# Layer norm root on ScalarE and centring on TensorE in the first layer of a two-layer kernel

## The chip, the cores and the metric

The kernel runs on one core of a Trainium2 chip. The metric is the device time of one execution in microseconds, the median of three runs. A core has five engines that work side by side, each in its own program order: TensorE (PE in the profile; PEld is its weight load), VectorE (DVE), ScalarE (ACT), GpSimd (POOL) and SyncE (SP), which here only issues DMAs. They wait for each other at semaphores.

## The reference

The input x is 4 x 384 x 64 x 64 in float32. Two layers follow each other. The change is in the first.

```python
# layer 0: x = x + mamba(group_norm(x)); L = 64*64 tokens, C = 384, DI = 768, 16 states
xn = (xs - mu) * rsqrt(var + 1e-5)          # layer norm of the group norm's output, over C
xb, z = split(xn @ in_proj_w.T)             # 768 and 768
xc = silu(causal_conv4(xb) + conv_b)
dt, Bm, Cm = split(xc @ x_proj_w.T)         # 24, 16, 16
dt = softplus(dt @ dt_w.T + dt_b)
h = exp(dt * A) * h + dt * xc * Bm          # scan over L, 768 x 16 states
y = sum(h * Cm) + xc * D
out = (y * silu(z)) @ out_proj_w.T
# layer 1: x = x + outlook_attention(group_norm(x))
```

## The kernel before

The first layer (`mamba_layer`) cuts the 4096 tokens of each of the 4 images into 17 chunks of TM = 241 tokens, 68 in all. A chunk's scan is cut into NU = 12 units; each has 64 of the 768 channels, 16 states each, spread as 2 x 4 rows of 241 over 128 partitions. The program is one loop over the steps s, one unit each, written out by hand; every engine issues in exactly this order (`InOrder`). In step s:

- DVE does the second half of the inputs of unit s+1 (`s_inputs2`, h<-dxr,bp), then the two scans of unit s (`s_scan`, h<-da,h).
- ScalarE does the decays of unit s+1 (`s_decay`, da<-dtr,aneg, four exponentials into each of two PSUM tiles da0 and da1; a tile is free when the scan that reads it is done), with two small copies for the state.
- POOL multiplies unit s-1 with C (`s_outputs`, h<-h,bc), then makes the first half of the inputs of unit s+2 (`s_inputs`, h<-dxr,bc).
- In odd steps TensorE sums the states of units s-3 and s-2 (`s_sum`: y<-xc,ddiag and 16 products y<-h,ssum). The tile h has five buffers: the inputs that are written next, by POOL in the same step and by DVE in the step after, need a buffer that this sum has read.

Between these lies the front work of later chunks and the end work of an earlier one. The tables `plan` and `ends` say at which step r of a chunk, and in which of six slots of the step (EARLY, READY, SCAN, POOL, MID, LATE), each part is issued; r is counted from two chunks ahead, so that parts of several chunks meet in one step, and below "step 5" means s = 5 modulo 12. The front parts of a chunk are: f_load (x to xt); f_mean, f_center, f_square, f_var, f_root, f_pow, f_rs, f_scale (the norms); f_x, f_z (the input projection, ps_in, two blocks of 128 rows at a time); f_conv (four diagonal products per block, ps_cv); f_silu (two ACT_TABLE_LOADs around the silu of xc and zs); f_bc, f_xd (ps_xd, xd); f_dt (three products of 25 rows, ps_dt, each followed by an exponential, dt<-ps_dt); f_plog, f_dtx (the logarithm into PSUM, ps_lg, and dtx on DVE); f_log, f_spread, f_b. The end parts are e_load, e_project (ps_out, three times, copied to xr by ScalarE) and e_store.

All of these products share one PSUM pool, `pmm`, with the tag "mm" and two buffers: a product waits until the tile two before it has been read. The logarithm's tile ps_lg takes a turn in the same pool.

The group norm is folded into the layer norm: per image, `group_norm_coeffs` gives a scale sc and a bias bi for each channel, `x_coeffs` makes from them the matrix avs, the averaging matrix with its rows scaled by sc. f_mean multiplies xt with avs (three products that add up to the mean), f_center takes the mean from sc * xt on DVE, the bias is added within the square and within f_scale. f_root adds 1e-5 on DVE, f_pow raises to the power -0.5 on POOL, f_rs spreads the root over the partitions by a product, f_scale multiplies on DVE. The first chunk's parts run before the loop, the second chunk's are fitted into its first steps by `catch_up`.

Every operation of the first layer is recorded by one helper, so the profile has it at line 45; the groups are told apart by their tiles. The trace has two records for each float32 product.

Of the kernel before, what the change touches and what calls it, by code (L numbers as in the profile page):

```python
# [7 lines left out]
F32 = mybir.dt.float32  # L8
AF = mybir.ActivationFunctionType
# [3 lines left out]
P = 128  # L13
C = 384
# [65 lines left out]
def mamba_layer(ctx, tc, x, w, x1, sc1, bi1, consts, behind):  # L80
# [66 lines left out]
    def x_coeffs(b):  # L147


        st = [xstats[b][:, cb].rearrange("p a s -> p (a s)") for cb in range(NCB)]  # L150
        sc = small.tile([P, 1], F32, tag="sc0", name="sc0")
        bi = small.tile([P, 1], F32, tag="bi0", name="bi0")
        avs = small.tile([P, P], F32, tag="avs", name="avs")
        bc = small.tile([P, 1], F32, tag="bc0", name="bc0")

        def parts():
            yield from group_norm_coeffs(pe, ve, ae, gp, small, pmm, blk12, mhalf, st, sc, bi)
            ae.mul(avs, avg, sc)
            yield False
            pb = pmm.tile([P, 2, TM], F32, tag="mm", name="pb")  # L160
            pe.matmul(pb[:, 0, 0:1], avg, bi, start=True, stop=True)
            yield True
            ve.scalar_tensor_tensor(bc, pb[:, 0, 0:1], -float(NCB), bi, ALU.mult, ALU.add)

        norms.append([parts(), False])
        coeffs[b] = (sc, avs, bc)

    def norm_part(reads):

# [3 lines left out]
            if norms[0][1] is None:  # L173
                norms.pop(0)

    avg = load("avg", [P, P], wf)
    for i in range(NCB * NX):
        x_stat(0, i, x_load(0, i))

# [72 lines left out]
        if c.n < TM:  # L252
            gp.memset(c.xt[:, :, c.n : TM], 0.0)

    def f_mean(c):
        t = c.t
        c.sc, avs, c.bias = coeffs[c.b]
        c.ps = pmm.tile([P, 2, TM], F32, tag="mm", name="ps_ln")
        for cb in range(NCB):
            pe.matmul(c.ps[:, 0, :t], avs, c.xt[:, cb, :t], start=(cb == 0), stop=(cb == NCB - 1))  # L260

    def f_center(c, u=None):

        t = c.t
        c.u = front.tile([P, NCB, TM], F32, tag="u", name="u", bufs=2) if u is None else u
        ve.scalar_tensor_tensor(
            c.u[:, :, :t],
            c.xt[:, :, :t],
            c.sc,
            c.ps[:, 0:1, :t].to_broadcast([P, NCB, t]),  # L270
            ALU.mult,
            ALU.subtract,
        )

    def f_square(c):
        t, u = c.t, c.u
        c.sq = front.tile([P, NCB, TM], F32, tag="sq", name="sq")
        ae.activation(c.sq[:, :, :t], u[:, :, :t], AF.Square, bias=c.bias)

    def f_var(c):  # L280

# [10 lines left out]
    def f_root(c):  # L292
        n = c.spans[0][1]
        c.vs = front.tile([P, 2], F32, tag="vs", name="vs")
        ve.tensor_scalar_add(c.vs[:n, :], c.pv[:n, :, 0], 1e-5)

    def f_pow(c):
        n = c.spans[0][1]
        gp.tensor_tensor(c.vs[:n, :], c.vs[:n, :], mhalf[:n, :], ALU.pow)

    def f_rs(c):
        c.ps = pmm.tile([P, 2, TM], F32, tag="mm", name="ps_rs")
# [8 lines left out]

    def f_scale(c):
        t, u = c.t, c.u
        ve.scalar_tensor_tensor(
            u[:, :, :t],
            u[:, :, :t],
            c.bias,
            c.ps[:, 0:1, :t].to_broadcast([P, NCB, t]),
            ALU.add,
            ALU.mult,  # L320
        )

    def project(c, jj):
        t = c.t
# [146 lines left out]
    def at(f, *args):  # L471
        def part(c):
            f(c, *args)

        part.f = f
        return part

    plan = {
        (-12, SCAN): [f_load],
        (-10, EARLY): [f_mean],  # L480
        (-10, READY): [f_center],
        (-9, POOL): [f_square],
        (-7, EARLY): [f_var],
        (-7, MID): [f_root],
        (-6, SCAN): [f_pow],
        (-5, READY): [f_rs],
        (-5, SCAN): [f_scale],
        (6, MID): [at(f_x, 0)],
        (8, EARLY): [at(f_z, 0)],
        (8, MID): [at(f_x, 1)],  # L490
        (9, POOL): [at(f_z, 1)],
        (9, MID): [at(f_conv, 0)],
        (10, LATE): [at(f_z, 2)],
        (11, LATE): [at(f_x, 2)],
        (12, SCAN): [at(f_conv, 1)],
        (12, LATE): [at(f_conv, 2)],
        (13, POOL): [at(f_silu, "xc", "zs")],
        (14, POOL): [f_bc],
        (15, EARLY): [f_xd],
        (16, READY): [at(f_dt, 0)],  # L500
        (16, SCAN): [at(f_dt, 1)],
        (17, EARLY): [at(f_dt, 2)],
        (17, READY): [at(f_plog, 0)],
        (17, MID): [at(f_dtx, 0)],
        (18, EARLY): [at(f_plog, 1)],
        (18, SCAN): [at(f_dtx, 1), at(f_plog, 2)],
        (19, READY): [at(f_dtx, 2)],
        (19, POOL): [f_log],
        (19, MID): [f_spread],
        (22, SCAN): [f_b],  # L510
    }

    ends = {
        (-9, READY): [lambda c: e_load(c)],
        (4, READY): [lambda c: e_project(c, 0)],
        (6, EARLY): [lambda c: e_project(c, 1)],
        (6, POOL): [lambda c: e_project(c, 2)],
        (15, EARLY): [lambda c: e_store(c)],
    }

    def chunk(k):
        if k not in live:
            c = live[k] = Chunk()
            c.b, c.ci, c.t0, c.n = chunks[k]
            c.t, c.last = TM, live.get(k - 1)
        return live[k]


    def catch_up(s, when):
        for r, w in sorted(plan):  # L530
            n = 6 * r + w
            if 0 <= n < 6 * 20 and ((n - 40) * 23 // 41 if n < 81 else 23 + (n - 81) * 22 // 36) == 6 * s + when:
                for part in plan[r, w]:
                    f = getattr(part, "f", None)
                    if f is f_silu:
                        silu(first, "zs")
                    if f is not f_x:
                        part(second)
# [176 lines left out]
    w_taps(0, 2)  # L715
    f_mean(first)
    w_bias(0, 2)
    f_center(first)
    f_square(first)
    f_var(first)  # L720
    w_bias(2, 3)
# [10 lines left out]
    ve.reduce_sum(cws, cw, AX.X)  # L732
    ve.tensor_mul(cws, cws, bxz[:, :NJ])
    ve.tensor_add(cbias, cbias, cws)
    f_center(second)
    f_x(first, 1)
    f_square(second)
    f_conv(first, 0)
# [4 lines left out]
    f_rs(second)  # L743
    f_scale(second)
    f_conv(first, 1)
    f_mean(third)
    f_center(third, io.tile([P, NCB, XT], F32, tag="xr", name="u"))
    f_conv(first, 2)
    f_silu(first, "xc")
    f_square(third)  # L750
# [480 lines left out]
def layouts(inputs):  # L1231

    import numpy as np

    g = {k: np.asarray(v) for k, v in inputs.items()}
    c = np.ascontiguousarray

    def inner(v):
        v = v.reshape(NJ, P, *v.shape[1:])
        return c(np.swapaxes(v, 0, 1))  # L1240

    a = {}
# [24 lines left out]
    a["ident"] = np.eye(P, dtype=f)  # L1267
    a["avg"] = np.full((P, P), 1.0 / C, f)
# [26 lines left out]
```

## Time and profile before

| | us |
|---|---|
| median of 3 runs | 6304.97 (6302.08 to 6311.46) |
| profiled execution | 6291.97 |
| its span | 6289.9 |
| first scan starts, last scan ends | 111.2, 5031.1 |
| mean clock of TensorE, share of full | 0.936 |

The profiled execution is 13 us shorter than the median. Its span leaves out 2 us at the ends. The busy time of an engine is the union of its records; a busy PE need not be at its peak. In the view of groups a row ends with the idle time of the engine just before these instructions and with what ended it; in the timeline that stands in brackets.

### The profile page before, as it was taken

To read this page: it belongs to the slowest core of one execution; us is meant where nothing else is said; L and a number is where in the kernel's file an instruction comes from. 1 tells how busy PE (TensorE), PEld (TensorE's weight loads), DVE (VectorE), ACT (ScalarE), POOL (GpSimd) and SP (SyncE) were. 2 spreads that over 40 slices of the span, in tenths; PEclk is the share of its full clock that TensorE was granted. 3 is DMA by queue.
4 is the path that set the end of the run, shared out by engine and by line. 5 is a ranking of instruction groups with operands and counts; after the bars stand their busy time and mean duration, and the time that the engine had idled before them with its cause. 6 is when DMAs were issued, how large, how long until landed. Compare 5 with 4: busy or idle time off the path is not lost. (4 is left out here: it accounts for less than half of the span.)

```text
span 6289.9 us, 113342 instructions
## 1 busy us (share of the span) xinstructions
PE 5605.3 (89%) x40488; PEld 3949.3 (63%) x40488; DVE 5373.2 (85%) x4783; ACT 4985.3 (79%) x11842; POOL 5310.6 (84%) x2047
## 2 busy tenths in 40 slices
PE   6888888898888888888888888998888789999999
PEld 5666666666666666666666666666666455555555
DVE  4999999999999999999999999999999945544444
ACT  3888888888888889888888988889988744445453
POOL 3999999999999999999999999999999933333333
PEclk9999999999989899999999999999999799999999
DMA  4555555555555555545555455555555634455444
GB/s 128 133 136 146 147 132 137 129 133 143 147 132 139 138 133 143 139 130 146 135 145 149 127 135 132 134 139 133 130 132 130 176 132 167 162 172 170 170 163 143
DMA packets 639978, 894.21 MB, mean 142 GB/s; under 512 B 130153, under 2 KB 533915, under 8 KB 639284
## 3 DMA queue, kind: packets, MB, share of 16 engines
q1 hardware_dynamic: 639412, 886.96, 51.4%
q8 instruction: 319, 5.23, 0.4%
q14 instruction: 247, 2.02, 0.1%
HBM read 660.89 MB, written 225.70 MB: 141 GB/s over the span
## 5 line engine op out<-in xcount | busy, mean ns | idle before, releaser
L45 DVE TENSOR_TENSOR_SCAN h<-da,h 128x968 f32<-128x968 f32 x1632 | 3449.1, 2154 | 82.6 <-issue 53.7
L45 ACT ACTIVATE da<-dtr,aneg 128x241 f32<-128x241 f32 x6528 | 3036.5, 465 | 294.2 <-DVE h L45 131.5
L45 POOL TENSOR_TENSOR h<-h,bc 128x1928 f32<-128x1928 f32 x816 | 3231.0, 3960 | 12.3 <-DVE h L45 10.1
L45 POOL TENSOR_TENSOR h<-dxr,bc 128x964 f32<-128x964 f32 x816 | 1628.1, 1995 | 104.7 <-PE y L45 88.0
L45 PE MATMUL ps_in<-u,win 128*128 128x241 f32 x4896 | 1078.6, 374 | 85.9 <-DVE dtx L45 78.8
L45 PEld LDWEIGHTS ps_in<-u,win 128*128 128x128 f32 x4896 | 911.0, 190 | 251.4 <-DVE dtx L45 102.9
L45 POOL TENSOR_TENSOR bd<-ain,own 99x1188 f32<-99x1188 f32 x192 | 413.0, 2180 | 744.9 <-DMA ain<-ad 504.9
L45 DVE TENSOR_TENSOR h<-dxr,bp 128x964 f32<-128x964 f32 x816 | 928.1, 1137 | 101.4 <-PE y L45 87.2
L45 PE MATMUL y<-h,ssum 128*32 128x241 f32 x13056 | 906.1, 405 | 23.8 <-POOL h L45 22.6
L45 PEld LDWEIGHTS y<-h,ssum 128*32 128x32 f32 x13056 | 433.0, 119 | 440.9 <-issue 215.4
L45 PE MATMUL ps_cv<-xb,cdiag 128*128 128x241 f32 x3264 | 694.3, 368 | 6.4 <-ACT neg L45 4.3
L45 PEld LDWEIGHTS ps_cv<-xb,cdiag 128*128 128x128 f32 x3264 | 611.0, 189 | 79.9 <-issue 13.5
L45 PE MATMUL ps_xd<-xc,wx 128*56 128x241 f32 x816 | 304.6, 554 | 322.9 <-ACT xc L45 322.9
L45 PE MATMUL psv<-wv,xp 128*128 128x384 f32 x1728 | 589.3, 492 | 0.8 <-ACT vst L45 0.8
L45 ACT ACTIVATE bd<-ain,own 99x324 f32<-99x324 f32 x704 | 334.6, 555 | 293.9 <-PE ps L45 282.5
L45 PE MATMUL ps_out<-zs,wout 128*128 128x241 f32 (+1 forms) x2448 | 536.6, 368 | 0.0
L45 DVE TENSOR_TENSOR fold<-fold,ps 128x192 f32<-128x192 f32 (+1 forms) x768 | 210.9, 303 | 341.1 <-PE ps L45 328.0
L45 PEld LDWEIGHTS ps_out<-zs,wout 128*128 128x128 f32 x2448 | 469.1, 192 | 36.6
L45 PEld LDWEIGHTS psv<-wv,xp 128*128 128x128 f32 x1728 | 320.5, 190 | 224.5 <-issue 7.5
L45 PEld LDWEIGHTS ps_xd<-xc,wx 128*56 128x56 f32 x816 | 153.5, 197 | 462.9 <-ACT xc L45 348.4
L45 PE MATMUL ps_dt<-xd,wdt 25*128 25x241 f32 x816 | 251.5, 434 | 114.4 <-ACT dt L45 80.9
L45 PE MATMUL y<-xc,ddiag 128*128 128x241 f32 x816 | 278.9, 426 | 9.5 <-DVE zs L45 9.5
(108 smaller groups left out, 5342.9 us busy)
## 6 DMA issues: line engine op xcount, KB each, us to landing
dxr<-dxd SPq DMA_DIRECT2D x1632, 120.5 KB
dtr<-dtd SPq DMA_DIRECT2D x1632, 120.5 KB
bc<-bcd SPq DMA_DIRECT2D x544, 120.5 KB
vin<-vd SPq DMA_DIRECT2D x384, 148.5 KB
vd<-vst SPq DMA_DIRECT2D x93, 576.0 KB
dxd<-dtx SPq DMA_DIRECT2D x272, 180.8 KB
dtd<-dt SPq DMA_DIRECT2D x272, 180.8 KB
xs<-in_x SPq DMA_DIRECT2D x96, 256.0 KB
```

Of the source, the lines that this page charges most:

```text
L45: return self.tc.keep_in_program_order(issue(*args, **kwargs))
```

## The change

The mean is no longer taken away on DVE. For each of the three blocks of channels TensorE makes the centred and scaled value whole: the block's own matrix `own` (identity less average, rows scaled by sc) times its part of xt, plus the matrix `others` (minus the average, scaled) times the two other parts. That is nine products in two PSUM tiles (two blocks and one), which ScalarE fetches into u with the bias added. The square and the scaling lose their bias; the scaling is a plain product. The 1e-5 and the root become a logarithm with the bias eps and an exponential with the scale -0.5, both on ScalarE. The order of parts in `plan` and `ends`, and the formula of `catch_up`, are changed as well.

```diff
-            ae.mul(avs, avg, sc)
+            ae.mul(others, navg, sc)
+            ae.mul(own, cavg, sc)
...
-    def f_mean(c):
-        c.sc, avs, c.bias = coeffs[c.b]
-        c.ps = pmm.tile([P, 2, TM], F32, tag="mm", name="ps_ln")
-        for cb in range(NCB):
-            pe.matmul(c.ps[:, 0, :t], avs, c.xt[:, cb, :t], start=(cb == 0), stop=(cb == NCB - 1))
-    def f_center(c, u=None):
-        ve.scalar_tensor_tensor(
-            c.u[:, :, :t],
-            c.xt[:, :, :t],
-            c.sc,
-            c.ps[:, 0:1, :t].to_broadcast([P, NCB, t]),
-            ALU.mult,
-            ALU.subtract,
-        )
+    def f_mean(c, part=None):
+        for n in (0, 1) if part is None else (part,):
+            own, others, c.bias = coeffs[c.b]
+            c.ps = pmm.tile([P, 2, TM], F32, tag="mm", name="ps_ln")
+            for cb in range(2 * n, min(NCB, 2 * n + 2)):
+                for i in range(NCB):
+                    pe.matmul(
+                        c.ps[:, cb % 2, :],
+                        own if i == cb else others,
+                        c.xt[:, i, :TM],
+                        start=(i == 0),
+                        stop=(i == NCB - 1),
+                    )
+            if part is None:
+                f_center(c, n)
+    def f_center(c, n):
+        cbs = slice(2 * n, min(NCB, 2 * n + 2))
+        ae.activation(c.u[:, cbs, :TM], c.ps[:, : 2 - n, :], AF.Identity, bias=c.bias)
     def f_square(c):
-        ae.activation(c.sq[:, :, :t], u[:, :, :t], AF.Square, bias=c.bias)
+        ae.activation(c.sq[:, :, :t], u[:, :, :t], AF.Square)
     def f_root(c):
-        ve.tensor_scalar_add(c.vs[:n, :], c.pv[:n, :, 0], 1e-5)
+        ae.activation(c.vs[:n, :], c.pv[:n, :, 0], AF.Ln, bias=eps[:n])
     def f_pow(c):
-        gp.tensor_tensor(c.vs[:n, :], c.vs[:n, :], mhalf[:n, :], ALU.pow)
+        ae.activation(c.vs[:n, :], c.vs[:n, :], AF.Exp, scale=-0.5)
     def f_scale(c):
-        ve.scalar_tensor_tensor(u, u, c.bias, c.ps ..., ALU.add, ALU.mult)
+        ve.tensor_mul(u[:, :, :t], u[:, :, :t], c.ps[:, 0:1, :t].to_broadcast([P, NCB, t]))
...
     plan = {
-        (-12, SCAN): [f_load],
-        (-10, EARLY): [f_mean],
-        (-10, READY): [f_center],
-        (-9, POOL): [f_square],
+        (-11, READY): [f_load],
+        (-10, EARLY): [at(f_mean, 0)],
+        (-10, READY): [at(f_center, 0), at(f_mean, 1)],
+        (-10, POOL): [at(f_center, 1)],
+        (-8, READY): [f_square],
         (-7, EARLY): [f_var],
-        (-7, MID): [f_root],
-        (-6, SCAN): [f_pow],
+        (-7, READY): [f_root],
+        (-7, SCAN): [f_pow],
...
-        (6, MID): [at(f_x, 0)],
+        (7, MID): [at(f_x, 0)],
...
-        (9, MID): [at(f_conv, 0)],
-        (10, LATE): [at(f_z, 2)],
-        (11, LATE): [at(f_x, 2)],
+        (9, MID): [at(f_z, 2)],
+        (10, LATE): [at(f_conv, 0)],
+        (11, MID): [at(f_x, 2)],
         (12, SCAN): [at(f_conv, 1)],
-        (12, LATE): [at(f_conv, 2)],
-        (13, POOL): [at(f_silu, "xc", "zs")],
-        (14, POOL): [f_bc],
-        (15, EARLY): [f_xd],
+        (12, MID): [at(f_conv, 2)],
+        (14, READY): [at(f_silu, "xc", "zs")],
+        (15, READY): [f_bc],
+        (15, SCAN): [f_xd],
         (16, READY): [at(f_dt, 0)],
         (16, SCAN): [at(f_dt, 1)],
-        (17, EARLY): [at(f_dt, 2)],
+        (16, MID): [at(f_dt, 2)],
         (17, READY): [at(f_plog, 0)],
-        (17, MID): [at(f_dtx, 0)],
-        (18, EARLY): [at(f_plog, 1)],
+        (17, MID): [at(f_dtx, 0), at(f_plog, 1)],
...
-        (19, POOL): [f_log],
         (19, MID): [f_spread],
+        (19, LATE): [f_log],
...
     ends = {
-        (-9, READY): [lambda c: e_load(c)],
-        (4, READY): [lambda c: e_project(c, 0)],
-        (6, EARLY): [lambda c: e_project(c, 1)],
+        (-9, LATE): [lambda c: e_load(c)],
+        (4, EARLY): [lambda c: e_project(c, 0)],
+        (6, READY): [lambda c: e_project(c, 1)],
         (6, POOL): [lambda c: e_project(c, 2)],
-        (15, EARLY): [lambda c: e_store(c)],
+        (14, READY): [lambda c: e_store(c)],
     }
```

More of the change, by code (lines that the diff above doesn't have):

```diff
@@ L152, in x_coeffs @@
         bi = small.tile([P, 1], F32, tag="bi0", name="bi0")
-        avs = small.tile([P, P], F32, tag="avs", name="avs")
+        others = small.tile([P, P], F32, tag="others", name="others", bufs=1)
+        own = small.tile([P, P], F32, tag="own", name="own", bufs=1)
         bc = small.tile([P, 1], F32, tag="bc0", name="bc0")
@@ L157, in parts @@
             yield from group_norm_coeffs(pe, ve, ae, gp, small, pmm, blk12, mhalf, st, sc, bi)
-            ae.mul(avs, avg, sc)
+            ae.mul(others, navg, sc)
+            ae.mul(own, cavg, sc)
             yield False
             pb = pmm.tile([P, 2, TM], F32, tag="mm", name="pb")
-            pe.matmul(pb[:, 0, 0:1], avg, bi, start=True, stop=True)
+            pe.matmul(pb[:, 0, 0:1], navg, bi, start=True, stop=True)
             yield True
-            ve.scalar_tensor_tensor(bc, pb[:, 0, 0:1], -float(NCB), bi, ALU.mult, ALU.add)
+            ve.scalar_tensor_tensor(bc, pb[:, 0, 0:1], float(NCB), bi, ALU.mult, ALU.add)
         norms.append([parts(), False])
-        coeffs[b] = (sc, avs, bc)
+        coeffs[b] = (own, others, bc)
     def norm_part(reads):
@@ L174, in norm_part @@
                 norms.pop(0)
-    avg = load("avg", [P, P], wf)
+    navg = load("navg", [P, P], wf)
+    cavg = load("cavg", [P, P], wf)
     for i in range(NCB * NX):
@@ L253, in f_load @@
             gp.memset(c.xt[:, :, c.n : TM], 0.0)
-    def f_mean(c):
-        t = c.t
-        c.sc, avs, c.bias = coeffs[c.b]
-        c.ps = pmm.tile([P, 2, TM], F32, tag="mm", name="ps_ln")
-        for cb in range(NCB):
-            pe.matmul(c.ps[:, 0, :t], avs, c.xt[:, cb, :t], start=(cb == 0), stop=(cb == NCB - 1))
-    def f_center(c, u=None):
-        t = c.t
-        c.u = front.tile([P, NCB, TM], F32, tag="u", name="u", bufs=2) if u is None else u
-        ve.scalar_tensor_tensor(
-            c.u[:, :, :t],
-            c.xt[:, :, :t],
-            c.sc,
-            c.ps[:, 0:1, :t].to_broadcast([P, NCB, t]),
-            ALU.mult,
-            ALU.subtract,
-        )
+    def f_mean(c, part=None):
[14 more added lines that the diff above has]
+    def f_center(c, n):
+        if n == 0 and c.u is None:
+            c.u = front.tile([P, NCB, TM], F32, tag="u", name="u", bufs=2)
+        cbs = slice(2 * n, min(NCB, 2 * n + 2))
+        ae.activation(c.u[:, cbs, :TM], c.ps[:, : 2 - n, :], AF.Identity, bias=c.bias)
     def f_square(c):
@@ L313, in f_scale @@
         t, u = c.t, c.u
[L314 to L321, printed above, removed]
+        ve.tensor_mul(u[:, :, :t], u[:, :, :t], c.ps[:, 0:1, :t].to_broadcast([P, NCB, t]))
     def project(c, jj):
@@ L524, in chunk @@
             c.b, c.ci, c.t0, c.n = chunks[k]
-            c.t, c.last = TM, live.get(k - 1)
+            c.t, c.last, c.u = TM, live.get(k - 1), None
         return live[k]
@@ L531, in catch_up @@
             n = 6 * r + w
-            if 0 <= n < 6 * 20 and ((n - 40) * 23 // 41 if n < 81 else 23 + (n - 81) * 22 // 36) == 6 * s + when:
+            if 0 <= n < 6 * 20 and ((n - 40) * 22 // 43 if n < 83 else 22 + (n - 83) * 23 // 34) == 6 * s + when:
                 for part in plan[r, w]:
@@ L717, in mamba_layer @@
     w_bias(0, 2)
-    f_center(first)
     f_square(first)
@@ L734, in mamba_layer @@
     ve.tensor_add(cbias, cbias, cws)
-    f_center(second)
     f_x(first, 1)
@@ L745, in mamba_layer @@
     f_conv(first, 1)
+    third.u = io.tile([P, NCB, XT], F32, tag="xr", name="u")
     f_mean(third)
-    f_center(third, io.tile([P, NCB, XT], F32, tag="xr", name="u"))
     f_conv(first, 2)
@@ L1267, in layouts @@
     a["ident"] = np.eye(P, dtype=f)
-    a["avg"] = np.full((P, P), 1.0 / C, f)
+    a["navg"] = np.full((P, P), -1.0 / C, f)
+    a["cavg"] = np.eye(P, dtype=f) - np.full((P, P), 1.0 / C, f)
     a["blk12"] = np.kron(np.eye(P // 4, dtype=f), np.full((4, 4), 1.0 / 12.0, f)).astype(f)
```

## The prediction

> **What bounds the kernel now.** I read the page's busy times first, then the busy time by stretch, then the totals of waits, then one chunk in order of time, last the granted clock in windows of that chunk. The change touches only the first layer: its 816 units, twelve to a chunk, run from about 111 to 5036 us.
>
> Page, busy times, and the steady stretch of the first layer by windows (columns: PE, PEld, DVE, ACT, POOL busy, clock, DMA):
>
> ```profile
> PE 5605.3 (89%) x40488; PEld 3949.3 (63%) x40488; DVE 5373.2 (85%) x4783; ACT 4985.3 (79%) x11842; POOL 5310.6 (84%) x2047
> ```
> ```profile
> 3000.00:4000.00 1000.00, 880.91 (x5816) 654.22 (x5815) 972.52 (x736) 898.50 (x2180) 988.55 (x355) 0.94 0.53 137
> ```
>
> In the stage that changes four engines are at 88 to 99%. POOL looks like the bound, so the square root that leaves it looks like the gain. The totals of waits (us, times, longest) speak against it:
>
> ```profile
> ACT da L45 <- DVE h L45: 131.5, 211, 3.9
> ...
> POOL h L45 <- PE y L45: 88.0, 91, 8.1
> DVE h L45 <- PE y L45: 87.2, 108, 6.3
> ...
> PE ps_in L45 <- DVE dtx L45: 78.8, 66, 5.3
> ```
>
> POOL itself waits for TensorE's sums y, once or more per chunk, and DVE waits for the same sums. A chain through several engines sets the pace. One chunk in order of time shows it:
>
> ```profile
> 3024.97 1.96 ACT L45 ACTIVATE da<-dtr,aneg 128x241 f32<-128x241 f32 x4 [0.65 <-DVE h L45]
> ...
> 3037.06 3.99 PE L45 MATMUL ps_xd<-xc,wx 128*56 128x241 f32 x12 [4.96 <-ACT xc L45]
> ...
> 3041.95 4.24 DVE L45 TENSOR_TENSOR_SCAN h<-da,h 128x968 f32<-128x968 f32 x2 [0.78 <-issue]
> ...
> 3051.81 0.56 ACT L45 ACTIVATE dt<-ps_dt 128x482 f32<-128x482 f32 x1
> ...
> 3052.42 1.08 PE L45 MATMUL ps_dt<-xd,wdt 25*128 25x241 f32 x4 [0.36 <-ACT dt L45]
> ...
> 3054.51 2.98 PE L45 MATMUL y<-h,ssum 128*32 128x241 f32 x32
> ...
> 3057.54 1.16 DVE L45 TENSOR_TENSOR h<-dxr,bp 128x964 f32<-128x964 f32 x1
> ...
> 3064.69 0.65 DVE L45 TENSOR_TENSOR dtx<-ps_lg,xc 128x482 f32<-128x482 f32 x1
> ...
> 3065.40 2.71 PE L45 MATMUL ps_in<-u,win 128*128 128x241 f32 x12 [1.14 <-DVE dtx L45]
> ...
> 3070.77 1.16 DVE L45 TENSOR_TENSOR h<-dxr,bp 128x964 f32<-128x964 f32 x1 [0.43 <-PE y L45]
> ...
> 3070.91 1.98 POOL L45 TENSOR_TENSOR h<-dxr,bc 128x964 f32<-128x964 f32 x1 [0.56 <-PE y L45]
> ...
> 3096.38 1.96 ACT L45 ACTIVATE da<-dtr,aneg 128x241 f32<-128x241 f32 x4 [0.66 <-DVE h L45]
> ```
>
> The loop, with medians over 52 chunks of the same timeline: (a) from the end of a chunk's first scan ScalarE runs without a pause, through the silu and its two table loads, to the second exponential of dt: 27.42 us. (b) TensorE then makes the third dt product and the sum of step 5: 1.86 + 4.07 (means 1.67 + 4.18 = 5.85). (c) DVE, released by that sum, goes from the input of step 6 to the third dtx: 7.81. (d) The third dtx frees the PSUM buffer for f_x(0), which stands ahead of the sum of step 7: 5.43 until DVE's next input. (e) DVE alone to the next chunk's first scan: 25.57. Together 72.2, and the median period is 72.0 us. POOL's own instructions start every 3.90 + 1.95 us back to back, 70.2 per chunk, 70.9 with the power of 0.70: it has 1.1 us of slack, which is its wait for y. DVE's instructions, start to start, make 69.6.
>
> **Off the loop: worth nothing while the loop holds.** POOL loses the power (702 ns, one per chunk); 0.66 us start to start, only more waiting for y. DVE loses the centring (955 ns) and the addition of 1e-5 (130 ns); both stand where it waits later anyway, for decays after the silu (0.78 us above) or for the sum of step 5. The scaling becomes a plain product of 723 elements; the row of 964 (1137 ns) gives 0.85, of 482 (646 ns) 0.97, against 0.94 now: no difference. TensorE makes nine centring products instead of three. Twelve records of ps_in start 2.4 us after each other, so a product costs 0.40, six 2.4; they lie in the 4.96 us in which it waits for the silu, and without that cover they would delay the sum of step 3, which has about 2.5 us to spare. The logarithm and exponential of 121x2 stand on ScalarE behind the end of (a); nearest row 128x3 at 297 ns, about 0.2 start to start, twice 0.4 at most, in front of decays that finish before DVE needs them, and ScalarE waits 1.27 us per chunk for ps_out just behind. Four more scalings of a 128x128 matrix, 0.39 each, are 1.6 us in all.
>
> **Steps moved without a price.** The load of x stands between the same two fetches on SP's queue. The silu and f_xd stay in the same gaps of (a), so their order changes and not its length. The store of dtd goes out behind the eight spreads (4.5 us of SP's time) instead of ahead of them, so the first dtr behind it now waits for its landing; the spreads no longer wait for the logarithm, which gives the time back. Were that not enough, decays would wait for dtr, which they do for 1.8 us in the whole run now. The projections f_z(2) and f_conv(0) change places inside one window of products. e_load is read a chunk later. The third dt product goes ahead of the variance, which matters below.
>
> **On the loop, per chunk.**
> 1. (a) gains the two fetches from PSUM. xb, 482 elements without a bias, takes 0.46 start to next; a bias adds 0.09 (zs 448 ns against xr 355, both 241), so 0.55; the second is like zs, 0.34. The square loses its bias, -0.09. Sum +0.80 (0.6 to 1.0 by the same rows with all or none of the overlap).
> 2. (b): the variance now stands between the second exponential and the sum of step 5, because it takes the PSUM buffer which that exponential frees. It costs 1.43 at full clock, 2.3 to 2.5 in the chunks whose records fall at half clock. The sum takes 2.35 at steps 7 and 9, 4.54 wholly at half clock. The window view, on the clock's own grid, shows why it is slow here:
>
> ```profile
> 3050.06:3053.47 3.41, 3.04 (x21) 2.29 (x19) 3.41 (x3) 3.25 (x9) 3.41 (x2) 1.00 0.89 232
> 3053.47:3056.89 3.42, 3.42 (x27) 1.63 (x30) 3.42 (x4) 3.29 (x8) 3.42 (x2) 0.50 0.84 218
> ```
>
> A window of dt products (25 rows) and variances (one column) is followed by one at half clock, though its records cover 3.04 of 3.41 us. In the new order the last full-array work, ps_out of step 4, starts sooner after the sum of step 3 and ends some 7 us before the sum of step 5; only dt and the variance lie between. That is two windows, so I put the variance at half clock (2.4) and the sum partly so (3.0 to 4.5, mid 3.85): 6.25 against 5.85, +0.40. Bounds: both at half 7.0, +1.2; both at full 3.8, where DVE's own row of work from the scan of step 3 (15.4 us) comes last instead, and (a) and (b) together end 0.3 earlier than now.
> 3. (d): f_x(0) is behind the sum of step 7, so the third dtx is followed by ps_rs and the sum (0.6 + 2.35), and DVE's two scans and scaling (4.15 + 0.87) come last: 5.03 against 5.43, -0.40.
> 4. (c) and (e) stay. From the sum of step 7 to that of step 9 TensorE now has 24 products for 18; 24 at 0.40 and the sum end 22.8 us after the input of step 6, DVE asks at 23.6.
>
> Sum: 0.80 + 0.40 - 0.40 = +0.80 us per chunk, 66 periods: +53. The start adds some 2 (six products at full or half clock 2.4 to 4.8, less the power, the addition and the centring, 1.8; the load of one more matrix). +55 on the profiled execution (span 6289.9, 6291.97 in all) gives 6347; the median of the runs stands 13 above that execution, so 6360.
>
> The Trainium skill, in TensorE: Matmul & The Clock Gate, Part 1, says that the clock halves after an idle window of about 3.4 us and returns after a busy one. Taken as a rule on idle time it would keep the window above at full speed, make the sum of step 5 2.35 us long, and the change would come out at about 44 us faster; the row at 0.50 decides for me.
>
> **Rivals.** First, the clock stays full at step 5, or the variance is done early: DVE's own row comes last, (a) and (b) -0.3, (d) -0.4, so -0.7 x 66 + 2 = -44, 6261. It decides if variance and sum take under about 4.7 us. Against it: all steady sums of step 5 take 3.75 to 4.54. Chance 0.13. Second, POOL is the bound after all: 0.66 x 66 = 44 less with its waits kept, up to 110 less if they go too (72.0 to 70.3). For it: 98.9% busy; against it: it waits in most chunks for a sum that does not wait for POOL. 0.05. Third, the three terms cancel within 0.2% (12.6 us, about what a measurement of this kernel tells from no change): 0.10. Fourth, the cold end: variance and sum all at half clock, or the sum of step 9 late by the 0.8 us that it has: 1.6 x 66 + 2 = +108, 6413; that is part of the forecast's side, in all 0.72. That the change does not do what it says is no rival: in the built order the power is gone from POOL, the nine products stand on TensorE and both fetches on ScalarE.
>
> The range goes from 6275, most of the way to the first rival, to 6410, near the cold end. Faster 0.18, same 0.10, slower 0.72.
>
> **What would show it.** Right: ScalarE's stretch (a) near 28.2; ps_var right behind the second dt exponential and at half clock; the sum of step 5 over 3.5 us; no ps_in waiting for dtx; POOL's and DVE's waits for y larger at step 5 and gone at step 7; a period near 72.8. Wrong: a period under 72 with the clock full at step 5, or POOL back to back at 70.3 without waits, or waits at step 9.

## The result and the profile after

| | before | after |
|---|---|---|
| median of 4 runs, us | 6303.52 (6295.44 to 6311.46) | 6400.2 (6399.19 to 6400.93) |
| profiled execution, its span, us | 6291.97, 6289.9 | 6399.19, 6397.4 |
| mean clock of TensorE | 0.936 | 0.925 |

The ratio is 1.0158, 95% interval 1.0145 to 1.0171: the change makes the kernel 97 us slower by the medians. The spans differ by 107.5 us; that is what the traces have to explain, since the profiled execution of before lies 12 us under its median and that of after does not. The last scan ends 108.2 us later than before and the second layer takes as long as it did, so all of it is in the first layer.

The page of after, busy times, and below it the steady stretch by windows (PE, PEld, DVE, ACT, POOL busy, clock, DMA):

```profile
PE 5759.4 (90%) x41304; PEld 4136.3 (65%) x41304; DVE 5303.0 (83%) x4647; ACT 5074.0 (79%) x12118; POOL 5265.8 (82%) x1979
```
```profile
3000.00:4000.00 1000.00, 894.85 (x5850) 676.95 (x5849) 933.64 (x690) 892.66 (x2175) 954.45 (x332) 0.92 0.51 134
```

POOL and DVE did lose work (45 and 70 us) and the kernel is slower: in the steady stretch they are busy for 954 and 934 of 1000 us where it was 989 and 973. The totals of waits of after say for whom they now wait (us, times, longest):

```profile
POOL h L45 <- PE y L45: 223.7, 78, 9.9
...
DVE h L45 <- PE y L45: 165.9, 79, 7.3
...
ACT xr L45 <- PE ps_out L45: 161.3, 76, 3.8
...
PE ps_var L45 <- ACT dt L45: 76.3, 64, 1.5
PE ps_rs L45 <- DVE dtx L45: 76.2, 63, 6.8
...
PE ps_xd L45 <- ACT u L45: 24.7, 3, 8.2
```

POOL's wait for the sums y went from 88.0 to 223.7 us, DVE's from 87.2 to 165.9. The row of ps_in that waited for dtx (78.8) is gone; ps_rs, which now stands first behind the third dtx, waits instead. The last row, three long waits, belongs to the starts of images. One chunk of after in order of time:

```profile
3020.88 1.96 ACT L45 ACTIVATE da<-dtr,aneg 128x241 f32<-128x241 f32 x4 [0.65 <-DVE h L45]
...
3038.43 4.24 DVE L45 TENSOR_TENSOR_SCAN h<-da,h 128x968 f32<-128x968 f32 x2 [2.22 <-issue]
3040.26 0.45 ACT L45 ACTIVATE u<-ps_ln,bc 128x241 f32<-128x241 f32 x1
...
3048.54 0.56 ACT L45 ACTIVATE dt<-ps_dt 128x482 f32<-128x482 f32 x1
...
3049.16 2.60 PE L45 MATMUL ps_var<-onesc,sq 128*121 128x1 f32 x12 [1.46 <-ACT dt L45]
...
3051.62 1.15 PE L45 MATMUL y<-xc,ddiag 128*128 128x241 f32 x2
...
3052.70 3.02 PE L45 MATMUL y<-h,ssum 128*32 128x241 f32 x32
...
3055.76 1.16 DVE L45 TENSOR_TENSOR h<-dxr,bp 128x964 f32<-128x964 f32 x1 [1.83 <-PE y L45]
3055.89 1.98 POOL L45 TENSOR_TENSOR h<-dxr,bc 128x964 f32<-128x964 f32 x1 [2.98 <-PE y L45]
...
3062.91 0.66 DVE L45 TENSOR_TENSOR dtx<-ps_lg,xc 128x482 f32<-128x482 f32 x1
...
3063.71 0.68 PE L45 MATMUL ps_rs<-ident,vs 121*128 121x121 f32 x4 [1.38 <-DVE dtx L45]
...
3068.42 1.16 DVE L45 TENSOR_TENSOR h<-dxr,bp 128x964 f32<-128x964 f32 x1
```

TensorE has nothing to do for 1.46 us until the second exponential of dt is done (3048.54 + 0.56). From there to DVE's next input (3055.76) the loop is TensorE's: the variance takes 2.60 us and the sum 4.1. In before the variance stood ahead of the third dt product and took 1.43:

```profile
3050.63 1.43 PE L45 MATMUL ps_var<-onesc,sq 128*121 128x1 f32 x12
3052.42 1.08 PE L45 MATMUL ps_dt<-xd,wdt 25*128 25x241 f32 x4 [0.36 <-ACT dt L45]
3053.43 1.16 PE L45 MATMUL y<-xc,ddiag 128*128 128x241 f32 x2
```

The clock in windows over the same place (the last window of 1.00 and the two behind it; clock is the column ahead of the DMA share):

```profile
3044.90:3048.31 3.41, 2.15 (x8) 1.32 (x8) 3.41 (x3) 3.31 (x9) 3.41 (x2) 1.00 0.77 204
3048.31:3051.73 3.42, 2.57 (x13) 2.57 (x13) 3.42 (x3) 3.04 (x8) 3.42 (x2) 0.50 1.06 234
3051.73:3055.14 3.41, 3.41 (x31) 1.57 (x34) 2.20 (x2) 3.25 (x10) 1.18 (x1) 0.50 0.96 221
```

In this chunk the variance and all but the last 0.6 us of the sum run at half clock, and POOL goes from 3.41 us busy in a window to 1.18. In the mean of 52 chunks TensorE spends 8.1 us at half clock between the first dt product and the end of the sum of step 5; before it was 5.4.

The loop of the prediction, medians over the same 52 chunks, means in brackets; (b) is parted into the time to the sum and the sum. Medians of parts need not add up: (b) as a whole is 6.26 (5.85) before and 7.03 (6.87) after.

| us per chunk | before | after |
|---|---|---|
| (a) first scan to second dt exponential | 27.42 (27.51) | 28.27 (28.74) |
| (b) from there to the sum of step 5 | 1.86 (1.67) | 2.51 (2.50) |
| (b) the sum | 4.07 (4.18) | 4.52 (4.36) |
| (c) DVE's input of step 6 to third dtx | 7.81 (7.85) | 7.81 (7.85) |
| (d) third dtx to DVE's next input | 5.43 (5.48) | 4.86 (4.91) |
| (e) to the next chunk's first scan | 25.57 (25.38) | 25.56 (25.35) |
| period | 72.01 (72.11) | 73.20 (73.75) |

Set against each other chunk by chunk from the ends of the first scans, the 108.2 us are: 6.7 until the first scan, 2.4 in the first period, 25.2 in the six periods around the starts of images 2 to 4, 76.0 in the other 60 periods (1.27 each), and -2.1 behind them.

### The profile page after: what moved, and what is told of

It is laid out like the page before. It is cut to its first block, busy times and chain, and to the rows that moved or that the text cites. A ratio compares the mean times of both kernels' runs of the same rounds, so it can differ in the third digit from the quotient of the medians.

```text
span 6397.4 us, 115178 instructions
## 1 busy us (share of the span) xinstructions
PE 5759.4 (90%) x41304; PEld 4136.3 (65%) x41304; DVE 5303.0 (83%) x4647; ACT 5074.0 (79%) x12118; POOL 5265.8 (82%) x1979
## 5 line engine op out<-in xcount | busy, mean ns | idle before, releaser
L45 POOL TENSOR_TENSOR h<-dxr,bc 128x964 f32<-128x964 f32 x816 | 1622.7, 1989 | 294.6 <-PE y L45 223.7
L45 DVE TENSOR_TENSOR h<-dxr,bp 128x964 f32<-128x964 f32 x816 | 931.9, 1142 | 175.7 <-PE y L45 165.9
L45 PE MATMUL ps_in<-u,win 128*128 128x241 f32 x4896 | 1060.0, 372 | 4.6 <-ACT xb L45 3.7
L45 PE MATMUL y<-h,ssum 128*32 128x241 f32 x13056 | 864.4, 410 | 14.6 <-POOL h L45 14.6
L45 PEld LDWEIGHTS y<-h,ssum 128*32 128x32 f32 x13056 | 416.3, 120 | 408.8 <-issue 232.5
L45 PE MATMUL ps_xd<-xc,wx 128*56 128x241 f32 x816 | 265.5, 496 | 228.1 <-ACT xc L45 203.4
L45 PEld LDWEIGHTS ps_xd<-xc,wx 128*56 128x56 f32 x816 | 135.1, 173 | 344.9 <-ACT xc L45 227.7
L45 PE MATMUL ps_dt<-xd,wdt 25*128 25x241 f32 x816 | 236.1, 417 | 39.0 <-ACT xr L45 33.6
```

The lines of the kernel that those rows point to most:

```text
L45: return self.tc.keep_in_program_order(issue(*args, **kwargs))
```

## The experiments

All times are medians in us. Each ratio is against runs of the kernel before that were made beside it, with its 95% interval.

**One part alone: f_x(0) behind the sum of step 7.**

```diff
-        (6, MID): [at(f_x, 0)],
+        (7, MID): [at(f_x, 0)],
```

> The kernel before with one line of the plan changed: f_x(0) behind the sum of step 7 instead of ahead of it. The loop theory: the stretch from the third dtx to DVE's next input falls from 5.43 to 4.9 us, POOL's waits for y at step 7 go, the chunk's period falls from 72.0 to 71.5, 30 to 36 us faster (ratio 0.994 to 0.996). Rival, POOL is the bound and its waits only move: same, within 6 us. Rival, the 24 products between the sums of steps 7 and 9 make the sum of step 9 late: slower, up to 30 us.

Measured 6289.58, ratio 0.9973 (0.9962 to 0.9983): a gain, about half of what was expected. (d) fell to 4.92, as it should; (b) grew from 5.85 to 6.23 by the means. Half-clock time between the first dt product and the end of the sum rose from 5.4 to 6.3 us. The half us that the move saves at step 7 is partly paid back at step 5.

**One part alone: the root on ScalarE, in its old slots.**

```diff
-        ve.tensor_scalar_add(c.vs[:n, :], c.pv[:n, :, 0], 1e-5)
+        ae.activation(c.vs[:n, :], c.pv[:n, :, 0], AF.Ln, bias=eps[:n])
...
-        gp.tensor_tensor(c.vs[:n, :], c.vs[:n, :], mhalf[:n, :], ALU.pow)
+        ae.activation(c.vs[:n, :], c.vs[:n, :], AF.Exp, scale=-0.5)
```

> The kernel before with the root alone changed: logarithm and exponential on ScalarE in the slots of the addition on DVE and of the power on POOL, centring and order as before. The loop theory: off the loop, period 72.0 as before, within 8 us of before; POOL's instructions are 0.66 us less per chunk and its waits for y at step 7 longer by about that. Rival, POOL is the bound: 0.66 x 66 = 44 us faster (ratio 0.993). Rival, ScalarE's busy time is the bound: two instructions of some 0.2 us, 26 us slower.

Measured 6411.47, ratio 1.0172 (1.0152 to 1.0192): a miss, and as slow as the whole change. Its loss is in (c), 7.85 to 9.61 by the means. Three totals of waits of this kernel show how (in before the first is 92.6 us, the second 5.7, and the third is not there):

```profile
ACT xr L45 <- PE ps_out L45: 257.4, 71, 4.6
...
DVE dtx L45 <- ACT ps_lg L45: 129.1, 62, 12.7
...
PE ps_out L45 <- ACT vs L45: 103.4, 64, 2.1
```

The logarithm at step 5, MID, stands on ScalarE behind decays. It is what frees the PSUM buffer of ps_var, and the ps_out of step 6 needs that buffer. So ps_out comes late, ScalarE waits for it with its copy to xr, the logarithms of dt behind that copy come late, and DVE waits for them with dtx. A tiny operation (0.26 us) on a fuller queue became the releaser of a shared buffer.

**The same, in the slots that the change gives it.**

```diff
-        (-7, MID): [f_root],
-        (-6, SCAN): [f_pow],
+        (-7, READY): [f_root],
+        (-7, SCAN): [f_pow],
```

> The kernel before with the root on ScalarE as in before_root, but in the slots of the changed kernel: the logarithm ahead of the first ps_lg, the exponential between the two decays of step 5. In before_root ps_out waited for ScalarE's logarithm, which held the PSUM buffer of the variance; here the buffer is free 2 us sooner. The loop theory: within 10 us of before. Rival, POOL is the bound: 44 us faster. Rival, the root on ScalarE is dear by itself: 100 us slower as before_root.

Measured 6305.13, ratio 1.0003 (0.9993 to 1.0013). POOL loses its power and its wait for y grows by about as much (0.80 to 1.54 us per chunk at step 7, 0.40 to 0.59 at step 5). That POOL bounds the kernel falls with this run, and the root is worth nothing, where its slot is right.

**The change without its centring**: group norm and centring back on DVE as before, with the new order of parts and the root on ScalarE. The lines of the plan, against the kernel after:

```diff
-        (-10, EARLY): [at(f_mean, 0)],
-        (-10, READY): [at(f_center, 0), at(f_mean, 1)],
-        (-10, POOL): [at(f_center, 1)],
+        (-10, EARLY): [f_mean],
+        (-10, READY): [f_center],
```

> The changed kernel with centring and folding of the group norm as before (three products for the mean, DVE centres, bias in square and scaling); the root on ScalarE and the new order stay. The loop theory against the changed kernel (6400): ScalarE's stretch from the first scan to the second dt exponential goes from 28.27 back to 27.4, and the two fetches no longer hold up the start of an image: 0.85 x 66 = 56 us, and 15 to 25 us for three image starts, 6320 to 6335. The variance behind the second dt exponential stays (2.5 us and a sum of 4.4 us at half clock), so it remains 15 to 35 us slower than before. Rival, the new order costs all of it: 6400. Rival, the centring was a gain and the order hid it: above 6400.

Measured 6336.27, ratio 1.0049 (1.0034 to 1.0064). The time is a microsecond above the range that was expected. The centring is 1.1% of the 1.6%. In the loop (a) is back at 27.72 and (b) stays at 2.51 + 4.52. That (a) does not come back to 27.42 is the order of parts: without the fetches ScalarE waits 0.20 us per chunk for scans within (a), in before 0.01. The last scan ends 60.6 us earlier than in after; 31.8 of these are in the 60 steady periods, 19.3 around the image starts, 9.5 at the start. So nearly half of what the centring costs is not in the loop.

**The change with the third dt product behind the variance again.**

```diff
-        (16, MID): [at(f_dt, 2)],
+        (17, EARLY): [at(f_dt, 2)],
```

> The changed kernel with one step moved back: the third dt product stands behind the variance again. The loop theory against the changed kernel (6400): between the second dt exponential and the sum of step 5 stand 1.1 to 2.0 us instead of 2.5; if the clock stays at half, the sum takes 4.1 to 4.5 as now; 0.5 to 1.4 us per chunk, 33 to 90 us faster, 6310 to 6367. Rival, busy time of the engines decides (nothing is removed): 6400. Rival, only the two fetches cost: 6400.

Measured 6358.65, ratio 1.0083 (1.0067 to 1.0099). This one line is worth 0.75%. (b) falls to 1.95 + 4.26 and the period to 72.91 (73.14 by the mean, 73.75 with the whole change). TensorE's rows of one chunk in order of time:

```profile
3023.82 1.08 PE L45 MATMUL ps_dt<-xd,wdt 25*128 25x241 f32 x4 [0.57 <-ACT xr L45]
3024.98 2.60 PE L45 MATMUL ps_var<-onesc,sq 128*121 128x1 f32 x12
3027.52 1.97 PE L45 MATMUL ps_dt<-xd,wdt 25*128 25x241 f32 x4
```

The variance is done in the time in which TensorE stood idle, in this chunk at half clock all the same (2.60; the median over the chunks is 1.84), and what is left behind the second exponential is here a dt product of 1.97 us and the sum. Most of the gain is that time to the sum, 1.95 for 2.50 by the means; the sum itself goes from 4.36 to 4.23.

**The change with its second fetch right behind the first.**

```diff
-        (-10, READY): [at(f_center, 0), at(f_mean, 1)],
-        (-10, POOL): [at(f_center, 1)],
+        (-10, READY): [at(f_center, 0), at(f_mean, 1), at(f_center, 1)],
```

> The changed kernel with the second fetch right behind the first, ahead of the silu, instead of behind the decays of step 2. At the start of an image the group norm's product takes a turn in the two PSUM buffers, so that ps_xd waits for the second fetch: periods of 79.5 and 76.7 us among 73.2, three times each in the run. The loop theory: these fall to some 74, 20 to 30 us in all; ScalarE's stretch keeps its length, so the other periods stay at 73.2; 6370 to 6380 against 6400. Rival, the group norm's own work makes these chunks long: 6400. Rival, the silu 0.35 us later delays the sum of step 3: above 6400.

Measured 6402.34, ratio 1.0160 (1.0146 to 1.0174): a miss. The image starts do become shorter (14.5 us above before where it was 25.2), the first scan starts 1.2 us later instead of 6.7, and no ps_xd waits for u any more; but the 60 other periods get 12 us longer together, since the second fetch now stands ahead of the silu and delays it ((a) 28.56 for 28.27). It cancels.

**Half of the sum taken off the path.** The first unit's eight products of the sum of step 5 go into step 4, behind ps_out; only the second unit's eight stay.

```diff
+    def s_early(u):
...
+        u.y = y = py.tile([P, TM], F32, tag="y", name="y")
+        pe.matmul(y[:, :t], ddiag[:, u.j, :], c.xc[:, u.j, :TM], start=True, stop=False, skip_group_check=True)
+        s_half(u, u, 0, False)
...
+                if m == 4 and (u := unit(s - 2)) is not None:
+                    s_early(u)
```

> The kernel before with the sum of step 5 cut in two: the D product and the half of the first of its two units go to step 4, in the pause behind ps_out, the half of the second stays. The loop theory: less of the sum stands behind the second dt exponential and the clock is more often full there; exponential to end of sum falls from 5.9 to 3 to 4.5 us, until DVE's own row of work comes last 0.7 us earlier; period 71.2 to 71.6, 25 to 50 us faster than before. Rival, the clock has no part and the chunk is bound by POOL: same. Rival, two halves of 16 records each take as long as one of 32: same or slower.

Measured 6268.72, ratio 0.9950 (0.9937 to 0.9963). From the second exponential to the end of the sum it takes 4.48 us for 6.26 (4.34 for 5.85 by the means), and DVE starts 0.56 later: its own row of work is last then. The sum of step 5 is on the path of before, as the prediction had it.

**The clock alone: more work for TensorE.** The kernel before, with products that it does not need: dt products of all 57 rows of xd (the first 32 against zeros), the variance in 64 columns, and three copies of the first product of the sum of step 5 early.

```diff
+    gp.memset(wdt[: 2 * NS, :], 0.0)
...
-                    pv[:n, i, 0:1], c.sq[:, cb, k0 : k0 + n], onesc, start=(cb == 0), stop=(cb == NCB - 1)
+                    pv[:n, i, :64], c.sq[:, cb, k0 : k0 + n], onesc.to_broadcast([P, 64]), start=(cb == 0), stop=(cb == NCB - 1)
...
-                pp[:, h, :t], wdt[2 * NS :, j * P : (j + 1) * P], xd[2 * NS : KX, 1:], start=True, stop=True
+                pp[:, h, :t], wdt[:, j * P : (j + 1) * P], xd[:KX, 1:], start=True, stop=True
...
+    def s_warm(u, n):
...
+        for _ in range(n):
+            pe.matmul(
+                u.y[:, :t], ddiag[:, u.j, :], c.xc[:, u.j, :TM], start=True, stop=False, skip_group_check=True
+            )
...
+        if m == 5 and (u := unit(s - 3)) is not None:
+            s_warm(u, 1)
...
+                if m == 4 and (u := unit(s - 2)) is not None:
+                    s_warm(u, 2)
```

> Kernel of before with work added on TensorE alone, the result the same: the dt products read all 57 rows of xd (the first 32 against zero weights) instead of 25, the variance is written in 64 columns instead of one, and the first product of the sum of step 5 is done early and four times instead of once (two copies while the second dt product waits, one behind the variance). The sum itself keeps its 16 products and its place. Theory (the clock at half makes the sum of step 5 long, and thin products call it): the granted clock around step 5 stays at 1.00, the sum takes 2.35 us or less instead of 4.1, DVE's own row comes last, period 71.2 to 71.7 instead of 72.0, ratio 0.993 to 0.997. Rival (the sum is long because POOL's products come late, and the added products only get in the way): no gain, or +0.4 us per chunk, ratio 1.000 to 1.004.

Measured 6243.52, ratio 0.9899 (0.9887 to 0.9912), more than expected. The chunk's TensorE rows in order of time, and the windows of the clock over them:

```profile
3084.44 0.98 PE L45 MATMUL y<-xc,ddiag 128*128 128x241 f32 x4
3085.69 1.08 PE L45 MATMUL ps_dt<-xd,wdt 57*128 57x241 f32 x4 [0.27 <-ACT dt L45]
3086.70 0.67 PE L45 MATMUL y<-xc,ddiag 128*128 128x241 f32 x2
3087.21 1.38 PE L45 MATMUL ps_var<-onesc,sq 128*121 128x64 f32 x12
3088.52 1.08 PE L45 MATMUL ps_dt<-xd,wdt 57*128 57x241 f32 x4
3089.53 0.68 PE L45 MATMUL y<-xc,ddiag 128*128 128x241 f32 x2
3090.14 1.84 PE L45 MATMUL y<-h,ssum 128*32 128x241 f32 x32
```
```profile
3084.07:3087.48 3.41, 3.14 (x17) 2.33 (x15) 3.41 (x2) 3.31 (x9) 3.41 (x2) 1.00 0.21 60
3087.48:3090.89 3.41, 3.41 (x33) 2.47 (x36) 3.41 (x4) 3.28 (x9) 3.41 (x3) 1.00 0.96 260
3090.89:3094.31 3.42, 1.75 (x27) 1.04 (x19) 3.42 (x5) 3.29 (x9) 3.42 (x2) 1.00 1.04 236
```

The first row is two of the copies, the row at 3086.70 the third. The clock stays at 1.00. The sum's 32 records take 1.84 us in all 52 chunks (3.18 in before, 88% of it at half clock), and no chunk has any half clock between the first dt product and the end of that sum. POOL is busy for 994 of 1000 us. The period is 71.28: DVE asks for its input 1.5 us after the sum is done, so DVE's own row now bounds the loop, as it does with the half sum.

**The rows alone**: of that diff only the line of zeros and the pair of the dt products.

> Kernel of before with one thing changed: the dt products read all 57 rows of xd, the first 32 against zero weights, instead of 25 rows; same number of instructions, same duration. If the clock goes by the share of the array in use, the rows alone lift the thin window, and the half-clock windows at step 5 become fewer: ratio 0.995 to 0.999. If it goes by idle time, nothing changes: 1.000.

Measured 6284.61, ratio 0.9968 (0.9956 to 0.9980). The products are as many and as long as before (1.08 us per pair). The half clock from the first dt product to the end of the sum of step 5 falls from 5.4 to 4.7 us per chunk, the period from 72.01 to 71.66 (72.11 to 72.00 by the means). The rows alone do part of it.

**The change with the clock held up**: the same additions to the kernel after, the three copies in the gap ahead of the variance.

> Kernel of after with the same work added on TensorE alone: dt products of 57 rows, variance in 64 columns, three copies of the first product of the sum of step 5 in the gap ahead of the variance. This puts the condition of the prediction's first rival (full clock at step 5) in force while ScalarE keeps its two fetches. Theory (the change loses by the clock at step 5, its 0.80 us on ScalarE being covered once that sum is short): the sum takes 2.35 us or less instead of 4.5, the variance 1.5 instead of 2.6, DVE's own row comes last, period 70.8 to 71.5, time 6245 to 6300, that is, as fast as before or faster. Rival (the fetches on ScalarE cost what they take, whatever the clock): period 72.2 or more, 6330 or more.

Measured 6287.24, ratio 0.9972 (0.9962 to 0.9982): the change, 1.6% slower as it stands, is faster than before once TensorE has more to do. The sum's records take 1.84 us in the median, (b) 5.12 instead of 7.03, the period is 71.64. In 41 of 52 chunks DVE still waits for that sum (0.33 us per chunk), so the longer (a) is not wholly covered. With the clock held up in both kernels, after stands 44 us above before (6287.24 and 6243.52, measured side by side). Up to the last scan the two differ by 46.9 us: 12.6 until the first scan, 2.4 in the first period, 17.8 around the image starts, 17.3 in the 60 steady periods (0.29 each), and -3.3 behind them. With the clock held up, the steady loop keeps little of the change's loss (0.29 of 1.27 us per period); the starts keep most of theirs.

**The centring alone, everything else in its old slot.** The root stays on DVE and POOL. The lines of the plan, against the kernel before:

```diff
-        (-10, EARLY): [f_mean],
-        (-10, READY): [f_center],
+        (-10, EARLY): [at(f_mean, 0)],
+        (-10, READY): [at(f_center, 0), at(f_mean, 1)],
+        (-10, POOL): [at(f_center, 1)],
```

> Kernel of before with the centring alone changed: nine products on TensorE, two fetches on ScalarE at step 2, the square without a bias, the scaling a plain product; the root stays on DVE and POOL, and every other part in its old slot. Theory (the fetches lengthen ScalarE's stretch from 27.4 to 28.2 and this ends last at the sum of step 5): period +0.7 to +0.9, start and image starts some +15 us, ratio 1.009 to 1.013. Rival (the loss of the change is in the new order of the parts, the fetches are covered): ratio 1.000 to 1.003.

Measured 6469.8, ratio 1.0255 (1.0242 to 1.0268): slower than the whole change, and a miss: about twice the loss that was expected. (a) is 29.69, not 28.2. A total of waits and two rows of one chunk of this kernel:

```profile
PE ps_xd L45 <- ACT u L45: 372.0, 64, 6.9
```
```profile
3073.99 0.66 ACT L45 ACTIVATE u<-ps_ln,bc 128x482 f32<-128x482 f32 x1
...
3074.69 4.91 PE L45 MATMUL ps_xd<-xc,wx 128*56 128x241 f32 x12 [5.21 <-ACT u L45]
```

In the old order the silu and both its table loads stand ahead of the first fetch on ScalarE. ps_xd takes the PSUM buffer that this fetch frees, so it starts behind the second table load, where it used to start behind the silu of xc. Everything that follows it is late, and ScalarE, which never paused in (a), waits 0.47 us per chunk for ps_xd and 0.97 for ps_out: 27.42 + 0.85 + 1.44 = 29.71, for 29.69 measured. With the new order of parts, the silu a step later, ps_xd waits for u only three times (24.7 us in the whole run); so it is the new order that keeps the centring from costing that, though the place of the silu alone was not run.

**The two gains together**: f_x(0) at step 7, the root on ScalarE in the new slots and the half sum, on the kernel before.

> The kernel before with three edits: f_x(0) behind the sum of step 7, the root on ScalarE as in before_root2, the sum of step 5 cut in two. The loop theory: DVE's own row of work and POOL's 70.2 us per chunk come last, period 70.4 to 71.0, 65 to 105 us faster than before (ratio 0.983 to 0.990). Rival, the clock's window takes back what the order gives, as it did in before_fx: 71.7, 20 us faster.

Measured 6222.19, ratio 0.9873 (0.9860 to 0.9887): the fastest of all, some 80 us under before, with the two parts of the change that cost nothing and one cut. Its period is 70.97.

## Why the prediction was right, and where its sizes were off

The direction and the mechanism hold: four engines at 88 to 99%, and yet the end is set by a chain whose links are ScalarE's stretch (a), TensorE's sum at step 5 and DVE's rows. The signs named at the end of the prediction are there but for the period: (a) 28.27 for 28.2; ps_var right behind the second exponential and at half clock (2.60); the sum 4.52; no ps_in waiting for dtx; POOL's wait at step 5 2.99 us per chunk for 0.40 and at step 7 0.10 for 0.80; DVE's for the same sums 2.12 for 0.76 and 0.04 for 0.47. The period, forecast near 72.8, is 73.20 (73.75 by the mean).

The total of 6360 is 40 us short, and 52 by the profiled executions (6347 and 6399.19): the 13 us that the forecast added for the median are not there in after. By the terms of the sum:

- (a): +0.80 forecast, +0.85 measured; the fetches take 648 and 444 ns, from start to next 0.65 and 0.34 where 0.55 and 0.34 were forecast.
- (b) is the term that was mis-sized: +0.40 forecast, +1.0 measured by the means (6.87 for 5.85), close to the cold end of +1.2. The time to the sum was put at 2.4 and is 2.5. The sum was put half-way between the clocks, at 3.85 (the middle of the bounds given, 3.0 and 4.5, is 3.75), and takes 4.36 in the mean and 4.52 in the median, which is half clock from end to end: the share of its 32 records at half clock is 93%. Either figure lies below the 4.18 that the sum took in before, and no row gave a reason for it to become shorter behind a variance at half clock; the forecast took it that the clock would come back within the sum, as it does in some chunks of before. The forecast also left out that the third dt product, moved away, leaves TensorE idle for 1.46 us ahead of the variance. That this idle time keeps the sum cold is not shown: with the product moved back the sum still takes 4.23, and the 0.75% of that run come mostly from the shorter time ahead of the sum.
- (d): -0.40 forecast, -0.57 measured. (c) and (e): 0, as forecast.
- Steps moved without a price: right for the store of dtd and the 24 products, not quite for the order in (a), which is 0.30 longer than in before even without the fetches (27.72). Decays wait for dtr once in the whole run (3.1 us, 1.8 before), and DVE does not wait at step 9 outside the image starts, so the 24 products there fit.
- Steady periods together: +1.27 each, over 60 of them 76 us, where +0.80 gives 48.
- Not in the sum: the starts of images 2 to 4, 25.2 us over six periods instead of 5. There the group norm's products take turns in the two PSUM buffers, so that ps_xd comes upon the buffer of the second fetch (the row of three waits, 8.2 us the longest). The run with the second fetch moved forward takes these waits away.
- The start: +6.7 to the first scan and 2.4 in the first period, instead of 2.

The first rival said that with the clock full at step 5 the change would be 44 us faster than before, 6261. The run that holds the clock up gives 6287.24, 0.28% faster: the mechanism and the sign of the rival are right, its time is 26 us short, and its condition is not given in the kernel as it is. The second rival, POOL as the bound, falls by the run with the root alone. The rule from the Trainium skill that the prediction weighed (TensorE: Matmul & The Clock Gate, Part 1: an idle window halves the clock) led to that rival's time. The row of the trace, a window of 3.41 us with 3.04 of records followed by half clock, led to the forecast, and the runs side with the row. As far as idle time goes the trace agrees with the rule, as the last section shows. What was measured lies between the forecast and the fourth rival, the cold end at 6413, and nearer to the latter. That the 108.2 us to the last scan meet the +108 of the cold end is luck: the 60 steady periods cost 20 us less than it says, the start and the image starts some 23 more. That the time lies in the range, 10 us below its upper end, is in part luck too: the 0.17 by which (d) came out better make some 11 us over 66 periods, and by them alone it is not above.

What the parts cost, by differences of ratios: centring 1.09% (1.0158 less 1.0049), the third dt product ahead of the variance 0.75%, the root 0.03%, f_x(0) -0.27%; together 1.60% against 1.58 measured. That the sum closes this well is partly chance, since the parts share the half-clock windows.

## What to carry to other kernels

When several engines are near full, follow one period in order of time and price each part at its place in the loop: here 45 us less of work on POOL and 70 on DVE were worth nothing, and 0.85 us per chunk on ScalarE, one product in another place and longer starts cost 1.6%. Where products share a small ring of PSUM buffers, moving one operation moves who frees whose buffer; ask for each slot which queue the releaser stands in, as a 0.26 us logarithm in the wrong slot cost 1.7%. Look at the granted clock in the windows ahead of every sum that others wait for; a few spare wide products there, or a part of the sum done early, can be worth more than the optimisation itself, as here (1.0% and 0.5% on the kernel before).

## What the runs showed of the hardware

The clock did not follow the time in which TensorE has records. In before a window of 3.41 us with 3.04 us of records, all of thin products (25 rows, or one column), was followed by one at 0.50; with 57 rows, 64 columns and a few full products a window with 3.14 us of records was followed by 1.00. Widening the dt products from 25 to 57 rows, at the same 1.08 us per pair, took 0.32% off the kernel by itself. The same shows over the whole first layer. From 300 to 5000 us of before, on the grid of the clock's windows, 90 windows at full clock hold 3.0 to 3.2 us of records. In 35 of them the dt and variance products fill more than half of that time, and 28 of these are followed by half clock; of the other 55 none is. With 57 rows alone 39 of 47 such windows still are, with the wider variance and the copies besides none of 21. Idle time counts as well: in before all 69 windows at full clock with less than 1.5 us of records are followed by half clock.

So what counts here is nearer to how much of the array is in use than to how long it is busy. The rows alone are the smaller part; the runs do not give the threshold, and they do not part the columns from the full products.

Work that is added can shorten a kernel: the kernel before with three needless products per chunk (1.65 us of records) and wider ones for the thin is 65 us faster. And a gain ahead of a half-clock window can be taken back by it: moving f_x(0) saved 0.5 us at step 7 and lost 0.4 at step 5, where the half-clock time rose from 5.4 to 6.3 us; why the windows fall so was not settled.
